# Where the sums' products stand on TensorE: between the two halves of a graph network's second layer

## The chip, the cores and the metric

The kernel runs on one NeuronCore of a Trainium2 chip. The metric is the device time of one execution in microseconds (us), taken as the median of several runs without a profile. Beside the runs there is one execution under the hardware profiler, and every duration of a single instruction comes from that one.

## The reference, cut to what matters

A graph has 6250 nodes with 128 features and 100000 edges that are sorted by destination. Each edge makes a message from its two nodes in three layers, the messages are averaged at their destination, and a small network and a layernorm update each node.

```python
msg_in = concatenate([x[src], x[dst]], axis=-1)      # (100000, 256)
h = relu(msg_in @ Wm1 + bm1)                         # first layer, 256
h = relu(h @ Wm2 + bm2)                              # second layer, 256
messages = h @ Wm3 + bm3                             # 128
agg = segment_sum(messages, dst, 6250) / clip(count, 1)
upd = relu(concatenate([x, agg], -1) @ Wn1 + bn1) @ Wn2 + bn2
out = layernorm(x + (x + upd))
```

The third layer is linear, so the kernel sums `h` over the edges of a node first and multiplies by `Wm3` only once a node.

## The kernel before, in words

There are three stages. A stage at the start multiplies every node's row by the two halves of `Wm1` and writes two tables to DRAM (`atab` for sources, `btab` for destinations). The edge loop, which takes most of the time, adds the two table rows of every edge, applies the second layer and adds the result up by node. A stage at the end multiplies the sums by `Wm3` and does the update and the layernorm.

The edge loop works on groups of 512 edges (`GE`), four tiles of 128 (`GT`); there are 196 groups (`NG`). It is software-pipelined by hand: loop step `i` fetches for group `i`, and with `g = i - ahead` (`ahead = 2`) does the following, for different groups, in this order.

- `fetch` (L358, L364): four indirect DMAs on POOL's queue bring rows of `atab` into `ag` (four buffers), four DMAs on SP's queue bring windows of `btab` into `bw` (four buffers). A buffer comes free when the first layer of an older group has read it.
- `hot` (L391, L394): VectorE makes the one-hot tiles `oht` (two buffers) and `oh` (four buffers) for the next first layer and for the sums.
- `add_up` for group `g - 4` (L447, L452): TensorE transposes `part` into `pt`, in tiles of 64 rows by 128 columns of its array; VectorE adds four windows of `pt` into the accumulator `acc`.
- `first_layer` for group `g` (L407, L413, L418): TensorE transposes the gathered source rows into PSUM (`ph`) and adds the destinations' rows through `oht` ("B's products", L413), also in tiles of 64x128; ScalarE applies bias and ReLU and writes `h1`.
- `sums` for group `g - 3` (L436, L439): TensorE multiplies four one-hot tiles by `h2`, each in a tile of 128 rows by 32 columns of the array, so the four stand side by side; the result `pg` (one buffer) is copied to `part` by ScalarE.
- `second_layer` for group `g - 1` (L427, L429): two halves of two edge tiles each. A half is four matmuls on the full 128x128 array into one of the two buffers of the tile `ph2`; VectorE's max with `-bm2` takes it out into `h2` (four buffers).

TensorE's instructions keep the order in which they are written (`manual_schedule`). The other engines' instructions are put in order by the framework's scheduler. Each matmul written in float32 shows up as two records in the profile: `L427` is written 1564 times and has 3128 records.

The names that follow below: L447, L407, L413, L436 and L427 are TensorE's five groups of instructions in one loop step, in the order before the change. In the profile the tiles `ph2` and `h2`, `h1` have lost their numbers and are called `ph` and `h`.

Of the kernel before, what the change touches and what calls it, by code (L numbers as in the profile page):

```python
# [27 lines left out]
def kernel(  # L28
# [41 lines left out]
    GT = 4  # L70
    GE = GT * P
    NG = -(-E // GE)
# [263 lines left out]
    def late_loads():  # L336
        nc.sync.dma_start(wu1, wn1.rearrange("(k p) h -> p k h", p=P))
        nc.sync.dma_start(wu2, wn2.rearrange("(k p) h -> p k h", p=P))
        nc.sync.dma_start(bu2[:, 0, :], bn2.rearrange("(o h) -> o h", o=1).to_broadcast([P, D]))

    with edge, tc.tile_pool(name="wk", bufs=2) as wk, tc.tile_pool(
# [7 lines left out]
        h2s = [wk.tile([P, GT, H + 1], F32, name=f"h2_{i}", bufs=1) for i in range(NH2)]  # L349
# [29 lines left out]
        def last_destinations():  # L379
            db = ld.tile([P, 2, 2 * P], I32, name="db", bufs=3)  # L380
            nc.vector.memset(db, NONE)
            nc.scalar.dma_start(db[:NQ, 0, :LAST], dst_row[:, NGF * GE:].to_broadcast([NQ, LAST]))
            return [db[:, 0, :]]
# [17 lines left out]
        def first_layer(ag, bw, oht, nt):  # L401
            nh = nt // 2
            phs = [p1.tile([P, HC, 2 * P], F32, name="ph") for _ in range(nh)]
            for c in range(HC):
                for u in range(GT):
                    for h in range(nh):
                        nc.tensor.matmul(phs[h][:, c, u * NQ:(u + 1) * NQ], ag[halves[h], u, c * P:(c + 1) * P],  # L407
                                         ident[halves[h], halves[h]], is_transpose=True,
                                         start=(c == 0 and u == 0), stop=False, skip_group_check=True)
            for c in range(HC):  # L410
                for k in range(2):
                    for h in range(nh):
                        nc.tensor.matmul(phs[h][:, c, k * P:(k + 1) * P], bw[halves[h], k, c * P:(c + 1) * P],  # L413
                                         oht[halves[h], k, :], start=False, stop=True, skip_group_check=True)
            h1 = wk.tile([P, HC, GE], F32, name="h1")
            for c in range(HC):
                for h in range(nh):
                    nc.scalar.activation(h1[:, c, h * 2 * P:(h + 1) * 2 * P], phs[h][:, c, :], AF.Relu,  # L418
                                         bias=b1[:, c:c + 1])
            return h1  # L420

        def second_layer(h1, h2, nt):
            for j0 in range(0, nt, 2):
                ph2 = p2.tile([P, 2, H], F32, name="ph2")
                for a in range(2):
                    for c in range(HC):
                        nc.tensor.matmul(ph2[:, a, :], h1[:, c, (j0 + a) * P:(j0 + a + 1) * P],  # L427
                                         w2[:, c, :], start=(c == 0), stop=(c == HC - 1))
                nc.vector.tensor_tensor(h2[:, j0:j0 + 2, :H], ph2, nb2.to_broadcast([P, 2, H]), op=ALU.max)  # L429

        def sums(oh, h2, nt):

            n = nt * WN
            pg = pa.tile([P, H + 1], F32, name="pg")
            for j in range(nt):
                nc.tensor.matmul(pg[j * WN:(j + 1) * WN, :], oh[:, j, :], h2[:, j, :],  # L436
                                 start=True, stop=True, skip_group_check=True)
            part = wk.tile([P, H + 1], F32, name="part")
            nc.scalar.copy(part[:n, :], pg[:n, :])  # L439
            return part  # L440
# [13 lines left out]
        def load_bases(ap, n, engine):  # L454
            _, firsts = nc.values_load_multi_w_load_instructions(
                ap[:, :n], engines=(engine,), min_val=0, max_val=N - 1,
                skip_runtime_bounds_check_because="the least of a window's destinations, or that "
                "and further windows, held to the nodes")
            return list(firsts)
# [4 lines left out]
        def double(t):  # L464
            n = min(P, N - t * P)
            nc.vector.scalar_tensor_tensor(x2[:n, t, :], x_sb[:n, t, :], 2.0, bu2[:n, 0, :],
                                           op0=ALU.mult, op1=ALU.add)

        ahead, lag = 2, 3
        st = {}  # L470
        for i in range(NG + ahead + lag + 1):
            if i == 16:
                late_loads()
                none = wk.tile([16, (NG * GE - E) // 16], I32, name="none", bufs=1)
                nc.vector.memset(none, NONE)
                nc.sync.dma_start(dpad[:E].rearrange("(p e) -> p e", p=16), dst.rearrange("(p e) -> p e", p=16))
                nc.sync.dma_start(dpad[E:].rearrange("(p e) -> p e", p=16), none)
            if 20 <= i < 20 + NT:
                double(i - 20)
            if i < NG:  # L480
                nt = GT if i < NGF else LT
                firsts = load_bases(tilei[0:1, i * GT:(i + 1) * GT], nt, ENG.SP)
                if i == NGF:
                    dbs = last_destinations()
                elif i % 2 == 0:
                    dbs = destinations(i, min(2, NGF - i))
                st[i] = dict(nt=nt, got=fetch(srcT[:, i, :], nt, firsts), db=dbs.pop(0))
            g = i - ahead
            if 0 <= g < NG:
                s = st[g]  # L490
                ag, bw = s.pop("got")
                oht, s["oh"] = hot(s.pop("db"), pbase[:, g, :], dloc[:, g, :s["nt"]], s["nt"])
            k = g - lag - 1
            if 0 <= k < NG:
                s = st.pop(k)
                if "firsts" not in s:
                    s["firsts"] = load_bases(tilei[0:1, k * GT:(k + 1) * GT], s["nt"], ENG.DVE)
                add_up(s["part"], s["firsts"], s["nt"])
            if 0 <= g < NG:
                s = st[g]  # L500
                s["h1"] = first_layer(ag, bw, oht, s["nt"])
            k = g - lag
            if 0 <= k < NG:
                s = st[k]
                s["part"] = sums(s["oh"], s["h2"], s["nt"])
            m = g - 1
            if 0 <= m < NG:
                s = st[m]
                s["h2"] = h2s[m % NH2]
                second_layer(s["h1"], s["h2"], s["nt"])  # L510
            if m == NG - 1:
                for k in range(NG - lag, NG):
                    s = st[k]
                    s["firsts"] = load_bases(tilei[0:1, k * GT:(k + 1) * GT], s["nt"], ENG.DVE)
# [10 lines left out]
        with tc.For_i(0, groups, 1) as g:  # L525
            more = nc.values_load(
                morei[0:1, ds(g, 1)], min_val=0, max_val=N // 16,
                skip_runtime_bounds_check_because="the difference of two nodes over 16")
            with tc.For_i(0, more, 1):
                for t, by in ((tilei[0:1, ds(g * GT, GT)], float(WB)), (pbase[:, ds(g, 1), :], float(WB)),  # L530
                              (dloc[:, ds(g, 1), :], -float(WB))):
                    nc.vector.tensor_scalar(t, t, by, None, op0=ALU.add)
                idx = wk.tile([P, GT], I32, name="idx")
                nc.vector.tensor_copy(idx, srcT[:, ds(g, 1), :].rearrange("p o j -> p (o j)"))
                pbc = wk.tile([P, 2], F32, name="pbc")
                nc.vector.tensor_copy(pbc, pbase[:, ds(g, 1), :].rearrange("p o k -> p (o k)"))
                dl = wk.tile([P, GT], F32, name="dl")
                nc.vector.tensor_copy(dl, dloc[:, ds(g, 1), :].rearrange("p o j -> p (o j)"))

                ti = wk.tile([1, GT], I32, name="ti")  # L540
                nc.vector.tensor_scalar_min(ti, tilei[0:1, ds(g * GT, GT)], float(N - 1))
                ag, bw = fetch(idx, GT, load_bases(ti, GT, ENG.SP))
                db, = destinations(g, 1, dpad_row)
                oht, oh = hot(db, pbc, dl, GT)
                h1 = first_layer(ag, bw, oht, GT)
                second_layer(h1, h2s[0], GT)
                add_up(sums(oh, h2s[0], GT), load_bases(ti, GT, ENG.DVE), GT)


# [128 lines left out]
```

## Time and profile before

| What | Value |
|---|---|
| median of 3 runs | 1224.58 us (1223.6 to 1225.11) |
| the profiled execution's own time | 1475.88 us |
| its span, first to last instruction | 1474.1 us |
| granted TensorE clock in it, mean | 0.981 |
| PE busy, share of the span | 1248.9 us, 85% |
| POOL busy | 814.5 us, 55% |
| DVE busy | 646.8 us, 44% |
| ACT busy | 440.6 us, 30% |
| PE's first and last second-layer matmul (L427) | 100.4 us and 1369.9 us after the start |

PE is TensorE's matmuls, PEld its weight loads, DVE VectorE, ACT ScalarE, POOL GpSimd, SP SyncE. A line of the timeline gives the start, the length from the first start to the last end of a merged stretch, the engine, the line of the kernel, what it writes and reads, and in brackets the idle time of that engine just before, with what ended it ("issue" is time in which the engine waited for nothing that the profile shows). The ends of matmuls are modelled, so distances from start to start are the ones to read.

The profiled execution is 251.3 us longer than the median of the runs.

### The profile page before, as it was taken

Reading aid. Unit: us, or ns where it says so; the run is one execution under the profiler, and the core shown is the slowest. Engines: PE = TensorE matmul, PEld = TensorE weight load, DVE = VectorE, ACT = ScalarE, POOL = GpSimd, SP = SyncE. Lnnn points to the kernel's source line nnn. Section 1 sums busy time; section 2 is a strip of 40 time slices with the busy share of each in tenths; the row PEclk is TensorE's granted clock in tenths of the full one; section 3 lists DMA queues with packets and bytes.
Section 4 is the critical chain, followed back from the end, with each engine's and each line's share of the span. In section 5 each row is a group of like instructions: output and inputs, shape, how many; then the busy total and the mean of one; then the engine's idle time right before and its main releaser. Section 6 shows DMA issues by size and latency. Waiting matters only on the chain. (4 is left out here: it accounts for less than half of the span.)

```text
span 1474.1 us, 32680 instructions
## 1 busy us (share of the span) xinstructions
PE 1248.9 (85%) x11192; PEld 918.8 (62%) x11193; DVE 646.8 (44%) x2086; ACT 440.6 (30%) x1142; POOL 814.5 (55%) x858
## 2 busy tenths in 40 slices
PE   7748888888888888888888888888888888889897
PEld 6626666666666666666666666666666666666555
DVE  6814443433434434444444444444444444444454
ACT  4512222222222222222222222222222222223244
POOL 7355655556556555655555555565555565563320
PEclk9959999999999999999999999999999999999999
DMA  9845444444444444444444444444444444442121
GB/s 275 288 160 136 119 121 125 120 125 118 118 127 123 120 128 115 121 128 123 120 123 120 122 127 125 119 125 116 123 126 121 124 124 116 124 122 59 47 68 54
DMA packets 158772, 184.06 MB, mean 125 GB/s; under 512 B 30214, under 2 KB 131994, under 8 KB 158588
## 3 DMA queue, kind: packets, MB, share of 16 engines
q0 software_dynamic: 37984, 103.35, 25.6%
q1 hardware_dynamic: 92056, 52.32, 12.1%
q10 hardware_dynamic: 28564, 26.27, 6.4%
q8 instruction: 90, 1.47, 0.4%
q14 instruction: 78, 0.64, 0.1%
HBM read 162.52 MB, written 19.68 MB: 124 GB/s over the span
## 5 line engine op out<-in xcount | busy, mean ns | idle before, releaser
L358 POOL DMA_INDIRECT ag<-atab,srcT x784 | 752.7, 960 | 527.9 <-PE ph L413 318.7
L427 PE MATMUL ph<-w,h 128*128 128x256 f32 x3128 | 735.0, 388 | 0.6 <-issue 0.4
L427 PEld LDWEIGHTS ph<-w,h 128*128 128x128 f32 x3128 | 582.9, 191 | 155.1 <-issue 56.9
L418 ACT ACTIVATE h<-ph,b 128x256 f32<-128x256 f32 x782 | 307.0, 475 | 931.2 <-PE ph L413 827.9
L429 DVE TENSOR_TENSOR h<-ph,nb 128x512 f32<-128x512 f32 x391 | 268.5, 692 | 692.9 <-PE ph L407 353.1
L413 PE MATMUL ph<-oht,bw 64*128 64x128 bf16 x1564 | 126.0, 217 | 188.4 <-issue 163.9
L413 PEld LDWEIGHTS <-bw 64*128 64x128 bf16 x1564 | 67.4, 94 | 232.0 <-issue 186.6
L452 DVE TENSOR_TENSOR acc<-acc,pt 128x63 f32 x782 | 172.2, 220 | 29.6 <-DVE acc L452 1.9
L407 PE MATMUL ph<-ident,ag 64*128 64x64 f32 x3128 | 134.2, 223 | 10.7 <-DMA ag<-atab,srcT 5.1
L436 PE MATMUL pg<-h,oh 128*32 128x257 f32 x1564 | 127.2, 394 | 1.5 <-issue 1.5
L407 PEld LDWEIGHTS ph<-ident,ag 64*128 64x128 f32 x3128 | 114.8, 140 | 10.5 <-DMA ag<-atab,srcT 5.6
L391 DVE TENSOR_SCALAR oht<-db,pbase 128x128 bf16<-128x128 int32 x392 | 104.5, 297 | 23.9 <-PE ph L413 18.5
L447 PEld LDWEIGHTS pt<-ident,part 64*128 64x128 f32 x1173 | 51.0, 136 | 66.7 <-issue 64.3
L439 ACT COPY part<-pg 128x257 f32<-128x257 f32 x196 | 76.8, 392 | 8.0 <-PE pg L436 8.0
L447 PE MATMUL pt<-ident,part 64*128 64x64 f32 x1173 | 77.9, 238 | 1.2 <-DVE acc L452 1.1
L582 POOL TENSOR_SCALAR const_part<-acc,b 128x512 f32<-128x512 f32 (+2 forms) x14 | 24.9, 1777 | 74.6 <-DVE agg L593 44.6
L394 DVE TENSOR_TENSOR oh<-iota_n,dloc 128x128 f32<-128x128 f32 x196 | 55.6, 285 | 5.3 <-PE pg L436 2.8
L226 PE MATMUL pbt<-w,xT 128*128 128x256 f32 x196 | 48.7, 395 | 2.8 <-ACT bt L235 1.9
L436 PEld LDWEIGHTS pg<-h,oh 128*32 128x32 f32 x1564 | 31.3, 108 | 22.9 <-issue 2.2
L226 PEld LDWEIGHTS pbt<-w,xT 128*128 128x128 f32 x196 | 36.5, 196 | 10.6 <-ACT bt L235 3.8
L586 PE MATMUL put<-xT,wu 128*128 128x512 f32 (+2 forms) x56 | 26.0, 590 | 2.8 <-issue 2.6
L246 POOL CAST bt<-rest 128x512 bf16<-128x512 f32 x18 | 12.8, 720 | 27.3 <-DVE rest L244 18.2
(99 smaller groups left out, 388.1 us busy)
## 6 DMA issues: line engine op xcount, KB each, us to landing
bw<-btab SPq DMA_DIRECT2D x782, 32.0 KB
db<-in_dst_dram ACTq DMA_DIRECT2D x194, 128.0 KB
ag<-atab,srcT POOLq DMA_INDIRECT x784
btab<-bt SPq DMA_DIRECT2D x24, 384.0 KB
atab<-bt SPq DMA_DIRECT2D x24, 256.0 KB
out_dram<-o SPq DMA_DIRECT2D x11, 256.0 KB
x_sb<-in_x_dram SPq DMA_DIRECT2D x5, 512.0 KB
rc<-rtab SPq DMA_DIRECT2D x10, 256.0 KB
```

Source lines behind the costliest of these rows:

```text
L226: nc.tensor.matmul(pbt[:, a, :], xT[:, (t0 + a) * P:(t0 + a + 1) * P], w1[:, k, :], start=True, stop=True)
L358: nc.gpsimd.indirect_dma_start(out=ag[:, j, :], out_offset=None, in_=atab[:, :], in_offset=bass.IndirectOffsetOnAxis(ap=idx[:, j:j + 1], a ...
L391: nc.vector.tensor_scalar(oht[:n, k, :], db[:n, k * P:(k + 1) * P], pb_cols[:n, k:k + 1], None, op0=ALU.is_equal)
L407: nc.tensor.matmul(phs[h][:, c, u * NQ:(u + 1) * NQ], ag[halves[h], u, c * P:(c + 1) * P], ident[halves[h], halves[h]], is_transpose=True, ...
L413: nc.tensor.matmul(phs[h][:, c, k * P:(k + 1) * P], bw[halves[h], k, c * P:(c + 1) * P], oht[halves[h], k, :], start=False, stop=True, ski ...
L418: nc.scalar.activation(h1[:, c, h * 2 * P:(h + 1) * 2 * P], phs[h][:, c, :], AF.Relu, bias=b1[:, c:c + 1])
L427: nc.tensor.matmul(ph2[:, a, :], h1[:, c, (j0 + a) * P:(j0 + a + 1) * P], w2[:, c, :], start=(c == 0), stop=(c == HC - 1))
L429: nc.vector.tensor_tensor(h2[:, j0:j0 + 2, :H], ph2, nb2.to_broadcast([P, 2, H]), op=ALU.max)
L436: nc.tensor.matmul(pg[j * WN:(j + 1) * WN, :], oh[:, j, :], h2[:, j, :], start=True, stop=True, skip_group_check=True)
L439: nc.scalar.copy(part[:n, :], pg[:n, :])
L447: nc.tensor.matmul(pt[:, c, :], rows, ident[halves[h], halves[h]], is_transpose=True, start=True, stop=True, skip_group_check=True)
L452: nc.vector.tensor_add(window, window, pts[j // 2][:, :, k:k + WB])
```

## The change

`second_layer` takes the tiles that it works on as an argument. In the edge loop it is called twice, for the first and the second two tiles, and `sums` is called between the two calls instead of ahead of both. Nothing is added or removed; on TensorE the eight `L436` records of a step move behind the first eight `L427` records.

```diff
-        def second_layer(h1, h2, nt):
-            for j0 in range(0, nt, 2):
+        def second_layer(h1, h2, tiles):
+            for j0 in tiles:
                 ph2 = p2.tile([P, 2, H], F32, name="ph2")
...
             if 0 <= g < NG:
                 s = st[g]
                 s["h1"] = first_layer(ag, bw, oht, s["nt"])
             k = g - lag
-            if 0 <= k < NG:
-                s = st[k]
-                s["part"] = sums(s["oh"], s["h2"], s["nt"])
             m = g - 1
             if 0 <= m < NG:
                 s = st[m]
                 s["h2"] = h2s[m % NH2]
-                second_layer(s["h1"], s["h2"], s["nt"])
+                second_layer(s["h1"], s["h2"], range(0, 2, 2))
+            if 0 <= k < NG:
+                s = st[k]
+                s["part"] = sums(s["oh"], s["h2"], s["nt"])
+            if 0 <= m < NG:
+                s = st[m]
+                second_layer(s["h1"], s["h2"], range(2, s["nt"], 2))
```

In the order of the built program, the scheduler answers on two other engines. On VectorE, `oh` (L394) moves from ahead of both maxima (L429) to between them. On ScalarE, the two DMAs that load `db` (L376), which are issued in every second step, move from behind the copy of `part` (L439) to ahead of it in most steps. POOL's and SP's order of work is the same.

## The prediction

> **What bounds the kernel now.** I read the page's busy table first: PE is busy for 85% of the span, POOL for 55%, the others for less. The windows view says that the edge loop is even from about 112 to 1372 us, with a granted clock of 1.00. So I looked at single loop steps of TensorE in the timeline. The first two that it has without a hole, one without sums and one with them:
>
> ```profile
> 106.87 0.72 PE L407 MATMUL ph<-ident,ag 64*128 64x64 f32 x16
> 107.42 0.39 PE L413 MATMUL ph<-oht,bw 64*128 64x128 bf16 x8
> 107.74 3.72 PE L427 MATMUL ph<-w,h 128*128 128x256 f32 x16
> 111.39 0.71 PE L407 MATMUL ph<-ident,ag 64*128 64x64 f32 x16
> 111.94 0.38 PE L413 MATMUL ph<-oht,bw 64*128 64x128 bf16 x8
> 112.26 0.64 PE L436 MATMUL pg<-h,oh 128*32 128x257 f32 x8
> 112.83 0.48 PE L427 MATMUL ph<-w,h 128*128 128x256 f32 x1
> ```
>
> See the distances from start to start: sums cost 0.57 us (112.26 to 112.83), the sixteen records of the second layer 3.65 us (107.74 to 111.39). A step in the middle of the loop looks like this:
>
> ```profile
> 726.98 0.40 PE L447 MATMUL pt<-ident,part 64*128 64x64 f32 x6
> 727.21 0.67 PE L407 MATMUL ph<-ident,ag 64*128 64x64 f32 x16
> 727.71 0.22 PE L413 MATMUL ph<-oht,bw 64*128 64x128 bf16 x1
> 728.09 0.21 PE L413 MATMUL ph<-oht,bw 64*128 64x128 bf16 x1 [0.17 <-issue]
> 728.82 0.35 PE L413 MATMUL ph<-oht,bw 64*128 64x128 bf16 x6 [0.51 <-issue]
> ```
>
> Here are holes of 0.17 and 0.51 us that end in "issue": nothing in the profile was waited for. Without holes a step is 0.23 (L447 to L407) + 0.50 (L407 to L413) + 0.32 (L413 to L436, from the stretch above) + 0.57 + 3.65 = **5.27 us**. In the profiled execution a step takes (1373.6 - 117.0)/195 = 6.44 us, from the first and the last start of L447, so 1.17 us of each are holes. The runs cannot have them: 195 x 6.44 = 1256 us is alone more than their 1224.58. Taking off the profiled execution's time around the loop, 117.0 + (1474.1 - 1373.6) + 1.8 = 219 us, leaves the runs (1224.6 - 219)/195 = 5.16 us a step. That is the step without holes within 2%, and the 0.1 us (20 us in all) is covered if the stages at the ends are a tenth faster in the runs. So the runs are bound by TensorE's own instructions, one behind the other, and the sum below is set against the median of the runs; the holes exist in the profiled execution alone.
>
> Does POOL bind? Four gathers a step:
>
> ```profile
> 730.64 0.95 POOL L358 DMA_INDIRECT ag<-atab,srcT  x1 [0.30 <-issue]
> 731.89 0.96 POOL L358 DMA_INDIRECT ag<-atab,srcT  x1 [0.30 <-issue]
> 733.16 0.95 POOL L358 DMA_INDIRECT ag<-atab,srcT  x1 [0.30 <-issue]
> 736.02 0.95 POOL L358 DMA_INDIRECT ag<-atab,srcT  x1 [1.91 <-PE ph L413]
> ```
>
> They stand 1.26 us apart, 5.04 us a step, and the first of each step waits for PE to free its `ag`. POOL is close behind, but it waits for PE, not PE for POOL: in the list of waits, L407 behind `ag` has 5.1 us in all.
>
> **What the Trainium skill says.** "TensorEngine Tiling (Array Packing)", Key Properties: "Changing tiling mode (not just tile) drains the TensorE"; it gives no price. "TensorE: Matmul & The Clock Gate", LDWEIGHTS: a weight load takes its columns over 1.2 GHz, 107 ns for 128 columns; the table at its head says that TensorE's queue pulls weight loads ahead of matmuls in flight. "Perfetto Trace Analysis", on the tensor engine's timeline: ends of matmuls are estimates, so I use starts. The trace agrees, with prices:
>
> ```profile
> 729.09 0.16 PEld L436 LDWEIGHTS pg<-h,oh 128*32 128x32 f32 x8
> 729.66 3.32 PEld L427 LDWEIGHTS ph<-w,h 128*128 128x128 f32 x16 [0.41 <-issue]
> 733.31 0.26 PEld L447 LDWEIGHTS pt<-ident,part 64*128 64x128 f32 x6 [0.33 <-issue]
> ...
> 729.98 3.40 PE L427 MATMUL ph<-w,h 128*128 128x256 f32 x15
> ```
>
> Where the tile changes (128*32 to 128*128, 128*128 to 64*128), the weight loads stop for 0.41 and 0.33 us. From L447 to L407, and from L407 to L413, where float32 gives way to bf16 but 64*128 stays, nothing stops. So it is the tile that drains. The last row starts at the second record: fifteen in 3.40 us, the last lasting 0.38, makes (3.40 - 0.38)/14 = 0.216 us from record to record, while the first (729.66) is 0.32 us ahead of the second. Right after a change of tile one weight load is not hidden: 0.104 us.
>
> **The change part by part.**
>
> - TensorE's changes of tile. Before, a step has three: L413 to L436, L436 to L427, L427 to L447. After, four: L413 to L427, L427 to L436, L436 to L427, L427 to L447. L413 to L427 is in the trace, 107.42 to 107.74 = 0.32, as dear as L413 to L436. L436 to L427 and L427 to L447 stay. New are (a) the drain L427 to L436, which the trace never shows. The nearest row is L427 to L447: the last record starts 3.65 - 0.32 - 14 x 0.216 = 0.31 us ahead, against 0.216 in a stream, so **0.094 us**. (b) The first half now pays the unhidden weight load, and the second half does too: one more, **0.104 us**. Together 0.198 us a step. Sums and second layer stand together in 194 steps (groups 3 to 196): 194 x 0.198 = **38 us**, all on the path, since nothing in the 5.27 us is idle to take it.
> - Bounds of (a): at least 0, if two tiles that both use 128 rows could follow each other without a drain; then only (b) stays, 20 us. At most the whole 0.31, if nothing of the last record overlapped: 80 us with (b), which the other three changes of tile don't suggest. I take 0.094.
> - VectorE: the max of the first half starts 0.57 us earlier behind L413, `oh` (0.28 us) stands between the maxima and waits for sums, which by then end 0.57 us after the first half. Its work in a step is 2 x 0.69 + 4 x 0.22 + 2 x 0.28 + 0.28 = 3.1 us of 5.27. Cost nothing; the cover is the 1.9 us of the second half. The first half waits for the older max of the same `ph2` buffer, the second half likewise; both are a step old.
> - ScalarE, counted from the start of L413: four activations begin at about 0.5 us and take 1.57, to 2.1; two issues of `db`, in every second step and now ahead of the copy, take 1.35, to 3.4; sums end at 0.32 + 1.93 (the first half with its drain) + 0.57 = 2.8, so the copy, 0.39, is done at 3.8 us with `db` and 3.3 without. The next L447, which waits for it, is due at 2.8 + 1.93 = 4.75. Cost nothing; 0.9 us of slack where there were two. If an issue of `db` waited for a landing by more than that, L447 would be late; the issue's own waits in the trace are under 0.05 us.
> - SP and POOL: `ag` and `bw` come free with L407 and L413, whose place is kept. Nothing, and POOL has 0.43 us of slack instead of 0.23.
>
> Sum: 1224.6 + 38 = **1263 us**. In the profiled execution the holes may swallow a part: its span should rise less than the runs do, if the holes come from the number of records in a step, which stays.
>
> **The rivals.**
>
> 1. Half the price: (a) is hidden, (b) stays: 1224.6 + 20 = 1245 us. For it: both tiles use all rows. Against it: L436 to L427, the same pair the other way, stops the loads for 0.41 us. Chance 0.10.
> 2. Not slower: PE has a hole in the runs that takes the 0.198. The place is L407, waiting for `ag`; the price is POOL's step. It decides from 5.46 us on, when a gather takes 1.365 us instead of 1.26; then the runs before were already bound by POOL at 195 x 5.46 = 1065 us and would have had only 160 us for the ends, where the profile has 219. Time then 1224.6. It speaks for it that POOL is within 5% of PE, against it that POOL waits for PE. Chance 0.07. Faster would need a stall of PE that the sums cover better in the second half's place. The one candidate is L427 waiting for the max, 22.3 us over 54 times in the list of waits, 0.41 each; but 0.41 is the drain that stands there in all other steps too, so nothing is left to win. Chance 0.03, some 1215.
> 3. Dearer: `part` comes late in the steps with `db`, or (a) costs up to 0.31: half the steps by 0.3 us is 30 us more, 1293. Chance 0.05.
>
> **How the numbers follow.** The likeliest case, 1263, has 0.75, with its own range of 1252 to 1272 (drain 0.04 to 0.14 us). Rival 1 brings the lower end to 1241; rival 2, faster and the top of rival 3 are left out, 0.15 together. A measurement of this kernel can tell about 0.2% from no change. Slower: 0.75 + 0.10 + 0.05 = 0.90; within: 0.07; faster: 0.03.
>
> **What would show it.** In the timeline after: L413 to L427 0.32 us; the eight records of the first half, then L436 at 0.32 + 6 x 0.216 + 0.31 = 1.93 us behind their start (1.83 would be rival 1); L436 to L427 0.57. The mean of an L427 record goes from 388 to about 394 ns, as two in sixteen are long; the weight loads of L436 get an idle time of 0.33 us each step. Wrong would be: no such idle time; L447 waiting for `part`; L407 waiting for `ag`; or runs under 1235 us.

## The result, and the profile after

The kernel after takes 1262.46 us, the median of 4 runs (1261.17 to 1263.27), beside 1224.39 us for the kernel before (1223.6 to 1225.11): a ratio of 1.031, with a 95% interval of 1.0292 to 1.0328. The change costs 38.1 us.

One thing must be known to read the rest. In all later sessions the kernel before itself took 1450 to 1473 us, and the one trace of it that was taken there has the same holes as the trace that the prediction read. Those sessions ran on chip 15 (e1 to e4), chip 6 (f1 to f3) and chip 2 (g1 to g4, and e7); on which chip the runs of 1224 us stood is not on record. Each experiment is therefore compared with the kernel before in its own session only.

The profiled execution of after has a span of 1259.9 us; its own time, 1261.65 us, is one of the four above. Its page, the busy line and the groups that the prediction spoke of (busy us, mean ns of one, idle time before):

```profile
PE 1219.0 (97%) x11192; PEld 881.5 (70%) x11193; DVE 666.4 (53%) x2086; ACT 460.9 (37%) x1142; POOL 808.9 (64%) x858
...
L427 PE MATMUL ph<-w,h 128*128 128x256 f32 x3128 | 780.4, 392 | 0.0
...
L407 PE MATMUL ph<-ident,ag 64*128 64x64 f32 x3128 | 132.0, 224 | 8.4 <-DMA ag<-atab,srcT 5.1
L436 PE MATMUL pg<-h,oh 128*32 128x257 f32 x1564 | 125.6, 392 | 0.0
...
L436 PEld LDWEIGHTS pg<-h,oh 128*32 128x32 f32 x1564 | 30.8, 108 | 64.5 <-issue 64.3
```

PE is busy for 97% of the span. The last row is the new change of tile: the weight loads of the sums now stand idle for 64.5 us in all, 0.33 us in each of 194 steps. In the page of before, the same row is:

```profile
L436 PEld LDWEIGHTS pg<-h,oh 128*32 128x32 f32 x1564 | 31.3, 108 | 22.9 <-issue 2.2
```

One step of TensorE in the timeline of after:

```profile
711.14 0.40 PE L447 MATMUL pt<-ident,part 64*128 64x64 f32 x6
711.38 0.66 PE L407 MATMUL ph<-ident,ag 64*128 64x64 f32 x16
711.88 0.39 PE L413 MATMUL ph<-oht,bw 64*128 64x128 bf16 x8
712.19 1.99 PE L427 MATMUL ph<-w,h 128*128 128x256 f32 x8
714.12 0.64 PE L436 MATMUL pg<-h,oh 128*32 128x257 f32 x8
714.69 1.99 PE L427 MATMUL ph<-w,h 128*128 128x256 f32 x8
716.61 0.40 PE L447 MATMUL pt<-ident,part 64*128 64x64 f32 x6
```

There is no hole. The distances are 0.24, 0.50, 0.31, 1.93, 0.57 and 1.92 us, together 5.47; the second layer, 3.65 us in one piece before, is 1.93 + 1.92 = 3.85 in two. The weight loads of the step before that one, where the second half now has a stop at each side and the sums have one ahead of them:

```profile
708.65 0.16 PEld L436 LDWEIGHTS pg<-h,oh 128*32 128x32 f32 x8 [0.33 <-issue]
709.22 1.59 PEld L427 LDWEIGHTS ph<-w,h 128*128 128x128 f32 x8 [0.41 <-issue]
711.14 0.26 PEld L447 LDWEIGHTS pt<-ident,part 64*128 64x128 f32 x6 [0.33 <-issue]
```

Over the loop it is (1160.8 - 104.0)/195 = 5.42 us from L447 to L447 on average, and 104.0 + (1259.9 - 1160.8) + 1.8 = 205 us around it. With the same 205 us the runs of before at 1224.39 us had (1224.39 - 205)/195 = 5.23 us a step. Each is about 0.05 us under its own distances (5.47 and 5.27), because the last steps of the loop have no first or second layer left to do. So the runs of before in that session had no holes either. No trace of such a run was taken; this is by subtraction, with the time around the loop taken from after. In the other traces that time is longer (217 to 237 us), which would leave even less room for holes.

### The profile page after: what moved, and what is told of

Same layout as the page of the kernel before. It is cut to its first block, busy times and chain, and to the rows that moved or that the text cites. A ratio compares the mean times of both kernels' runs of the same rounds, so it can differ in the third digit from the quotient of the medians.

```text
span 1259.9 us, 32619 instructions
## 1 busy us (share of the span) xinstructions
PE 1219.0 (97%) x11192; PEld 881.5 (70%) x11193; DVE 666.4 (53%) x2086; ACT 460.9 (37%) x1142; POOL 808.9 (64%) x858
## 3 DMA queue, kind: packets, MB, share of 16 engines
q0 software_dynamic: 37984, 103.35, 28.8%
## 5 line engine op out<-in xcount | busy, mean ns | idle before, releaser
L427 PE MATMUL ph<-w,h 128*128 128x256 f32 x3128 | 780.4, 392 | 0.0
L427 PEld LDWEIGHTS ph<-w,h 128*128 128x128 f32 x3128 | 563.2, 190 | 161.3 <-issue 80.0
L429 DVE TENSOR_TENSOR h<-ph,nb 128x512 f32<-128x512 f32 x391 | 270.7, 692 | 480.6 <-PE ph L427 475.2
L439 ACT COPY part<-pg 128x257 f32<-128x257 f32 x196 | 73.3, 374 | 194.3 <-PE pg L436 189.6
L407 PE MATMUL ph<-ident,ag 64*128 64x64 f32 x3128 | 132.0, 224 | 8.4 <-DMA ag<-atab,srcT 5.1
L436 PE MATMUL pg<-h,oh 128*32 128x257 f32 x1564 | 125.6, 392 | 0.0
L407 PEld LDWEIGHTS ph<-ident,ag 64*128 64x128 f32 x3128 | 114.2, 140 | 10.0 <-DMA ag<-atab,srcT 5.6
L391 DVE TENSOR_SCALAR oht<-db,pbase 128x128 bf16<-128x128 int32 x392 | 107.5, 355 | 9.1 <-PE ph L413 8.4
L447 PEld LDWEIGHTS pt<-ident,part 64*128 64x128 f32 x1173 | 51.2, 137 | 67.1 <-issue 64.0
L413 PE MATMUL ph<-oht,bw 64*128 64x128 bf16 x1564 | 76.9, 217 | 8.0 <-DMA bw<-btab 8.0
L447 PE MATMUL pt<-ident,part 64*128 64x64 f32 x1173 | 77.9, 238 | 1.6 <-ACT part L439 1.1
L436 PEld LDWEIGHTS pg<-h,oh 128*32 128x32 f32 x1564 | 30.8, 108 | 64.5 <-issue 64.3
L394 DVE TENSOR_TENSOR oh<-iota_n,dloc 128x128 f32<-128x128 f32 x196 | 61.3, 314 | 0.0
L413 PEld LDWEIGHTS <-bw 64*128 64x128 bf16 x1564 | 53.8, 96 | 8.6 <-DMA bw<-btab 8.6
```

Source lines behind the costliest of these rows:

```text
L391: nc.vector.tensor_scalar(oht[:n, k, :], db[:n, k * P:(k + 1) * P], pb_cols[:n, k:k + 1], None, op0=ALU.is_equal)
L447: nc.tensor.matmul(pt[:, c, :], rows, ident[halves[h], halves[h]], is_transpose=True, start=True, stop=True, skip_group_check=True)
```

## The holes: before once more, and after in a session with holes

The first experiment is the kernel before, unchanged.

> The kernel before, unchanged, once more under the profiler. The profiled execution of before had holes of 1.17 us in every loop step and a span of 1474 us, while that of after has none and a span of 1260 us with the same number of records. Theory A (the holes belong to this order of the work: about 5.27 us a step is more than the profiler can take away, 5.47 is not): the holes come again, a step takes about 6.4 us and the span is near 1474. Theory B (they were an accident of that one execution): no holes, 5.27 us a step, a span near 1223. The time without a profile stays at 1224 in both.

It took 1473.28 us, and 15 runs of the same kernel beside it 1472.49 us (1469.85 to 1475.19). A step took 6.44 us. Its timeline:

```profile
703.77 0.66 PE L407 MATMUL ph<-ident,ag 64*128 64x64 f32 x15
705.18 0.21 PE L407 MATMUL ph<-ident,ag 64*128 64x64 f32 x1 [0.76 <-issue]
705.89 0.42 PE L413 MATMUL ph<-oht,bw 64*128 64x128 bf16 x8 [0.50 <-issue]
706.24 0.64 PE L436 MATMUL pg<-h,oh 128*32 128x257 f32 x8
706.81 3.72 PE L427 MATMUL ph<-w,h 128*128 128x256 f32 x16
```

The holes come again, as theory A had it, and not by an accident of one execution: every run of the kernel in that session was as long. The expectation's last sentence, 1224 us for the runs, was wrong, and with it falls theory A's reason, the profiler: runs without a profile take as long. The next experiment asked whether after is spared; it is the kernel after, unchanged, in another session.

> The kernel after, unchanged, beside the kernel before. On the chip of the last four experiments the kernel before took 1472 us in 15 runs, with about 1.17 us of holes a step, and three other orders of the same work took 1457 to 1472: the holes belong to that chip, not to the profiler. Theory A: where the kernel before takes 1224 us, after takes 1262; where it takes 1472, the holes swallow the dearer changes of tile and after stays within 1450 to 1480. Theory B: this order of the work has no holes on any chip: 1262 us everywhere, and faster than before where before has them.

It took 1472.9 us (1466.63 to 1476.67) beside 1450.15 us for the kernel before: a ratio of 1.0166 (1.0139 to 1.0194). Theory B falls: this order has holes too. Two rows of PE's timeline in it, of one loop step:

```profile
703.71 0.46 PE L447 MATMUL pt<-ident,part 64*128 64x64 f32 x6 [1.87 <-issue]
...
705.28 3.13 PE L427 MATMUL ph<-w,h 128*128 128x256 f32 x8
```

A hole of 1.87 us stands ahead of L447, and the first half takes 3.13 us where it needs 1.99. Theory A holds in its range, but not that the change is free: 22.8 us of the 38 are left. That the holes belong to "that chip" is too narrow as well: f1 stood on another chip, and the next ones on a third.

## Moving the sums or the transposes, in sessions with holes

Three other orders of the same work stood in the session of e1. In the first the sums go behind both halves, and `add_up` a step later, so that the loop has one step more.

```diff
-            part = wk.tile([P, H + 1], F32, name="part")
+            part = wk.tile([P, H + 1], F32, name="part", bufs=3)
...
-            k = g - lag - 1
+            k = g - lag - 2
...
                 add_up(s["part"], s["firsts"], s["nt"])
...
-            k = g - lag
-            if 0 <= k < NG:
-                s = st[k]
-                s["part"] = sums(s["oh"], s["h2"], s["nt"])
...
                 second_layer(s["h1"], s["h2"], s["nt"])
+            k = g - lag
+            if 0 <= k < NG:
+                s = st[k]
+                s["part"] = sums(s["oh"], s["h2"], s["nt"])
```

> The sums stand behind both halves of the second layer, ahead of the next step's transposes (L447); the transposes of a group come one step later than before and part has three buffers, so that nothing waits for the copy. Theory (a change of tile is what costs): changes in a step are L413 to L427, L427 to L436, L436 to L447, three as in the kernel before, and one entry into the full tile. By the distances of the trace after, 0.234 + 0.500 + 0.317 + 3.652 + 0.571 = 5.274 us a step, the step of before: 1224 us, within 3. Rival (the sums must stand right behind L413; elsewhere VectorE's or ScalarE's part of the work comes late): it costs as after does or more, 1262 us.

In the second the sums go between `add_up` and `first_layer`.

```diff
                 add_up(s["part"], s["firsts"], s["nt"])
-            if 0 <= g < NG:
-                s = st[g]
-                s["h1"] = first_layer(ag, bw, oht, s["nt"])
             k = g - lag
             if 0 <= k < NG:
                 s = st[k]
                 s["part"] = sums(s["oh"], s["h2"], s["nt"])
+            if 0 <= g < NG:
+                s = st[g]
+                s["h1"] = first_layer(ag, bw, oht, s["nt"])
```

> The sums stand between the transposes of part (L447) and those of the gathered rows (L407), both in tiles of 64x128, with the second layer in one piece. Four changes of tile in a step as in after, but only one entry into the full 128x128 tile as in before. Theory (drain and unhidden weight load both cost): L447 to L436 0.327, L436 to L407 0.571, L407 to L413 0.55 (first after a change), L413 to L427 0.317, second layer 3.652: 5.417 us, 0.143 more than before, 194 steps: 1252 us. Rival (only the second entry into the full tile costs, the drain is free): 1224 us. Rival (a change costs the same whichever tiles it joins, 0.197): 1262 us.

In the third the whole block of `add_up` goes between the halves, and the sums keep their place.

```diff
-            k = g - lag - 1
-            if 0 <= k < NG:
...
-                add_up(s["part"], s["firsts"], s["nt"])
             if 0 <= g < NG:
...
-                second_layer(s["h1"], s["h2"], s["nt"])
+                second_layer(s["h1"], s["h2"], range(0, 2, 2))
+            k = g - lag - 1
+            if 0 <= k < NG:
...
+                add_up(s["part"], s["firsts"], s["nt"])
+            if 0 <= m < NG:
+                s = st[m]
+                second_layer(s["h1"], s["h2"], range(2, s["nt"], 2))
```

> The sums stay right behind L413 as before; the transposes of part (L447) with their adds stand between the two halves of the second layer instead of ahead of L407. Changes of tile in a step: L413 to L436, L436 to L427, L427 to L447, L447 to L427, L427 to L407: five instead of three, two entries into the full tile. Theory (changes of tile cost, whatever the instructions): 0.550 + 0.317 + 0.571 + 1.925 + 0.327 + 1.925 = 5.615 us, 0.341 more than before: 1291 us. Rival (what cost in after is the sums' own place, not the tile): 1224 us.

They took 1463.91 us (ratio to before 0.9943, 0.9927 to 0.996), 1456.52 us (0.9896, 0.988 to 0.9913) and 1471.65 us (0.9995, 0.9986 to 1.0004). No theory's number came out: a step takes 6.38, 6.33 and 6.43 us in the three, and 6.44 in before, while the distances without holes would be 5.27, 5.42, 5.62 and 5.27. The holes fill up most of what the order leaves. The first and the third were tried once more in the session of the kernel after:

> The sums behind both halves, the transposes of part a step later (part with three buffers), once more. Where the kernel before takes 1224 us, theory (changes of tile cost: three in a step, as before): 1224 us, within 3; rival (sums away from L413 cost): 1262 us. Where before takes 1472 us it took 1464 already and tells nothing.

> The transposes of part (L447) and their adds between the two halves, sums at their old place, once more. Where the kernel before takes 1224 us, theory (five changes of tile in a step, 0.341 us more): 1291 us; rival (only the place of the sums matters): 1224 us. Where before takes 1472 us it took 1472 already and tells nothing.

The first took 1448.01 us (0.9984, 0.9978 to 0.9991), the other 1459.68 us (1.0064, 1.0047 to 1.008), beside 1450.15 us. Again neither tells anything of the theories. What these five runs did give is a way out: holes that shrink when the work between them grows might be driven out by more work on PE.

## The same question with the second layer issued twice

In four kernels every second-layer matmul is issued twice. It is the change under study, its kernel before, and the two other places of the sums.

```diff
                 for a in range(2):
-                    for c in range(HC):
+                    for c in 2 * list(range(HC)):
                         nc.tensor.matmul(ph2[:, a, :], h1[...], w2[:, c, :], start=(c == 0), stop=(c == HC - 1))
```

> The order of before, with every second-layer matmul (L427) issued twice into the same place (the second pass overwrites the first with the same values). On the two chips of the runs so far the kernel before has holes of about 1.1 us a step that hide what a change of tile costs. A step's own distances become 5.27 + 16 x 0.216 = 8.73 us. Theory (the holes stand for a limit on how many of TensorE's instructions come by in a time; a step of 8.7 us with 61 written matmuls and loads is slower than that limit): no holes, 195 x 8.73 + 219 = 1921 us. Rival (the holes are latency that every step pays, about 1.1 us): 2130 us.

> The order of after, every second-layer matmul issued twice. Beside g1_twice_before this shows the change where no hole is in the way. Theory (one more drain, 0.094 us, and one more unhidden weight load, 0.104 us, in 194 steps): 38 us more than g1_twice_before. Rival (the cost in after came from somebody's lateness, which 3.45 us more of second layer would cover): the same as g1_twice_before within 4 us.

> The sums between the transposes of part (L447) and L407, every second-layer matmul issued twice. Four changes of tile like after, one entry into the full tile like before. Theory: 0.143 us a step more than before, 28 us more than g1_twice_before. If only the entry into the full tile costs: 0 to 4 us more. If every change costs the same 0.197 us: 38 us more.

> The sums behind both halves (transposes of part a step later, part with three buffers), every second-layer matmul issued twice. Three changes of tile, as before, but the sums are even further from L413 than in after. Theory (changes of tile cost): within 4 us of g1_twice_before. Rival (sums away from L413 cost, by VectorE or ScalarE being late): as g2_twice_after, 38 us more, or worse.

Measured in one session, in which the kernel before took 1450.71 us:

| Kernel | Median, range of its 4 runs | Against g1 | Expected |
|---|---|---|---|
| g1_twice_before | 1909.53 us (1909.35 to 1909.95) | | 1921 |
| g2_twice_after | 1949.41 us (1948.79 to 1949.72) | +39.9 | +38 |
| g3_twice_front | 1938.37 us (1937.23 to 1938.7) | +28.8 | +28 |
| g4_twice_last | 1911.02 us (1910.33 to 1911.67) | +1.5 | within 4 |

The ratios to the kernel before are 1.3155 (1.313 to 1.318), 1.3429 (1.3403 to 1.3454), 1.3351 (1.3326 to 1.3377) and 1.3165 (1.314 to 1.319). The holes are gone; a hole in every step would have made 2130 us of g1. The start of one step in g1's timeline:

```profile
1005.88 0.40 PE L447 MATMUL pt<-ident,part 64*128 64x64 f32 x6
1006.12 0.66 PE L407 MATMUL ph<-ident,ag 64*128 64x64 f32 x16
1006.62 0.39 PE L413 MATMUL ph<-oht,bw 64*128 64x128 bf16 x8
1006.93 0.64 PE L436 MATMUL pg<-h,oh 128*32 128x257 f32 x8
```

The distances are those that the prediction used: 0.24, 0.50, 0.31. Doubling the second layer adds 3.45 us of work to a step but only (1909.53 - 1450.71)/195 = 2.35 us of time; about 1.1 us was hole. The weight loads of g2 show the same two stops around the sums as those of after, and the one behind the second half:

```profile
1005.18 0.16 PEld L436 LDWEIGHTS pg<-h,oh 128*32 128x32 f32 x8 [0.33 <-issue]
1005.76 3.32 PEld L427 LDWEIGHTS ph<-w,h 128*128 128x128 f32 x16 [0.41 <-issue]
1009.41 0.26 PEld L447 LDWEIGHTS pt<-ident,part 64*128 64x128 f32 x6 [0.33 <-issue]
```

What follows: the change costs its 38 to 40 us where lateness of others is covered (g2, in which a step leaves VectorE and ScalarE 3.45 us more than in after). Moving the sums further away than after did costs 1.5 us, with one loop step more, as long as the changes of tile stay three (g4). Its order, behind both halves:

```profile
1005.00 0.64 PE L436 MATMUL pg<-h,oh 128*32 128x257 f32 x8
1005.57 0.40 PE L447 MATMUL pt<-ident,part 64*128 64x64 f32 x6
1005.80 0.67 PE L407 MATMUL ph<-ident,ag 64*128 64x64 f32 x16
```

And the price is that of the tiles joined, not one for every change: a fourth change that doesn't enter the full tile costs 28.8 us (g3). In g3 the sums are followed by L407 instead of a second entry into the full tile:

```profile
1003.76 0.40 PE L447 MATMUL pt<-ident,part 64*128 64x64 f32 x6
1004.08 0.64 PE L436 MATMUL pg<-h,oh 128*32 128x257 f32 x8
1004.65 0.71 PE L407 MATMUL ph<-ident,ag 64*128 64x64 f32 x16
1005.20 0.39 PE L413 MATMUL ph<-oht,bw 64*128 64x128 bf16 x8
```

From L447 to L407 directly is 0.24 us; over the sums it is 0.32 + 0.57, of which 0.57 had been paid at the old place too, so that 0.09 is new (before rounding it is 0.327 against 0.234); and L407, now first behind a change, takes 0.55 instead of 0.50. Together that is 0.14 us a step, 28 us in 194.

## A version meant to beat both

If changes of tile cost, the sums of two groups should share one visit to their tile.

```diff
-        name="pa", bufs=1, space=PSUM
+        name="pa", bufs=2, space=PSUM
...
-            oh = wk.tile([P, GT, WN], F32, name="oh", bufs=4)
+            oh = wk.tile([P, GT, WN], F32, name="oh", bufs=6)
...
-            part = wk.tile([P, H + 1], F32, name="part")
+            part = wk.tile([P, H + 1], F32, name="part", bufs=4)
...
-            k = g - lag - 1
+            k = g - lag - 2
...
-            k = g - lag
-            if 0 <= k < NG:
-                s = st[k]
-                s["part"] = sums(s["oh"], s["h2"], s["nt"])
+            for k in (g - lag - 1, g - lag):
+                if g % 2 == 0 and 0 <= k < NG:
+                    s = st[k]
+                    s["part"] = sums(s["oh"], s["h2"], s["nt"])
```

> A version that should beat both: the order of before, but the sums of two groups stand together behind L413 in every second step (two buffers of pg, four of part, six of oh, adds a step later). Every second visit to the 128x32 tile is saved. By the distances: a step without sums 0.234 + 0.500 + 0.317 + 3.652 = 4.70 us, one with two 5.274 + 0.43 = 5.71, mean 5.21, 0.066 less than before. Where the kernel before takes 1224 us (no holes): 1211 us. Where it takes 1450 to 1472 (holes of about 1.1 us a step): TensorE's instructions are as many as before and the holes swallow it, within 0.5% of before.

It took 1481.63 us (1476.55 to 1483.89) beside 1472.79 us for the kernel before in that session: a ratio of 1.0052 (1.0037 to 1.0067), at the edge of the 0.5% that was expected. In its timeline a pair of sums without a hole inside costs 711.31 - 710.25 = 1.06 us, where 0.57 + 0.43 = 1.00 was expected, and holes stand ahead of it:

```profile
709.51 0.21 PE L413 MATMUL ph<-oht,bw 64*128 64x128 bf16 x1 [0.73 <-issue]
710.25 1.13 PE L436 MATMUL pg<-h,oh 128*32 128x257 f32 x16 [0.53 <-issue]
711.31 1.99 PE L427 MATMUL ph<-w,h 128*128 128x256 f32 x8
```

So a gain was not shown, and where holes set the time this version is slightly slower. What it takes in a session without holes was not tried.

## Why the prediction was right, point by point, and where it was not

- **TensorE's own instructions bound the runs.** Right: from 112 to 1160 us PE is busy for 1046.9 of 1048 us in after, and L407 waits for `ag` no longer than before (5.1 us in all). The prediction's 5.16 us a step came out 0.1 us under its own sum for two reasons: the time around the loop was 205 us and not 219, and the mean over the loop takes in the last, shorter steps.
- **(a), the drain from L427 to L436, 0.094 us.** Right. In after the weight loads stop for 0.33 us there, as ahead of L447, and L436 comes 1.93 us behind the half's first record, the distance forecast; 1.83 would have been no drain. This was a price read at another pair of tiles and carried over, and it fitted.
- **(b), the second unhidden weight load, 0.104 us.** Right: 3.85 - 3.65 = 0.20 us is (a) and (b) together. g3 has a fourth change without a second entry and costs 28.8 us, not 39.9. What the traces show is that the second record comes 0.104 us late. That a weight load of the 107 ns that the prediction quotes is left unhidden there is its reading: in before the second load does start 0.11 us after the first (729.66 and 729.77), but the profile gives each load a length of 190 ns.
- **The sum.** 194 x 0.198 = 38 us forecast, 38.1 measured.
- **Nothing is late on VectorE and ScalarE.** Right. In the step of after that is shown above, which has `db`, the copy of `part` ends at 714.99 + 0.38 = 715.37 and the next L447 starts at 716.61: 1.24 us of slack, where 0.9 was forecast.

```profile
714.99 0.38 ACT L439 COPY part<-pg 128x257 f32<-128x257 f32 x1 [1.07 <-PE pg L436]
```

- **The same by experiment.** The weight loads of L447 wait for `part` for 3.1 us in the whole kernel after, and g4, with the sums elsewhere, is not late either.
- **"The holes exist in the profiled execution alone."** Wrong. Every run of the kernel before in the later sessions was as long as one with holes, while the profiled execution of after, under the same profiler, has none and is as fast as its runs. The step that failed is the reasoning that 251 us between the profiled execution and the runs must come from the profile; that the two came from different sessions is likely, but not on record. The sum survived because it was set against the runs and used distances without holes, and also by luck: the result was taken where before has no holes. In the session of f1 the same change costs 22.8 us and not 38.
- **"Its span should rise less than the runs do."** Wrong for the same reason: the span fell from 1474.1 to 1259.9 us. But the thought behind it, that holes swallow a part of the price, is what f1 shows.
- **Rival 2, a hole in the runs that takes the price,** was given 0.07 and tied to POOL. With holes the change does cost less, 22.8 us; but the holes shown end in "issue" and not in a wait for `ag`.
- **The mean of an L427 record** is 392 ns, 394 was forecast.

## What to carry to other kernels

On TensorE the order of groups had a price of its own in this kernel where neighbours use different tiles of the array: count the changes of tile in a loop step, and count the entries into the full tile once more. Only float32 groups, and one in bf16, were seen here; other types and tiles have to be read anew. The price is read from the timeline without any run, as the distance from the last record of one tile to the first of the next, less the distance in a stream, plus what the second record is late. Where the profiled execution and the runs are far apart, take a second profile before giving the difference a cause; and where holes hide an effect, add work to the bound engine in both versions and compare those.

## What the runs showed of the hardware that was not expected

- The same program took 1224 us in the first session and 1450 to 1473 us in the later ones. In the slower ones TensorE has holes of 1.1 to 1.2 us a step that end in "issue". The mean granted clock differs little: 0.973 to 0.986 in the runs of the sessions with holes that don't issue the second layer twice, 0.987 to 0.989 in the four runs of after in the first session; for the runs of 1224 us none is on record. The holes vanish when a step of the same program has 8.7 us of TensorE work (g1). That is consistent with a limit on TensorE's instructions in a time: a step has 108 records, 54 of matmuls and 54 of weight loads (a float32 transpose, L407 or L447, is one record; only the float32 products are two), so 6.44/108 = 60 ns each with holes, while g1, with 140, takes 8.73/140 = 62 ns without. But after in the first session took 5.42/108 = 50 ns each, so such a limit would have to differ between the sessions; and with as many records as before, after took 22.8 us longer in the session of f1 and e7 0.5% longer in its own. The number of the chip alone doesn't settle it: in its two sessions on chip 2 the kernel before took 1450.71 and 1472.79 us. The cause stays open.
- Between two groups in different tiles the drain is nearly the same in the three pairs where it can be read, 0.09 us: L427 to L447 and L427 to L436 (0.31 where a stream has 0.216), and L447 to L436 (0.327 where L447 to L407, in one tile, has 0.234). What stands behind the change differs: the second record of L427 in the full tile is 0.104 us late, and L407 in tiles of 64x128 takes 0.05 us more. That these are weight loads which the change leaves unhidden was not tested apart.
